# The second table of a graph network made within the first convolution's loop

## The chip, the cores and the metric

The kernel runs on one core of a Trainium2 chip. The metric is device time of one launch in microseconds (us). Five engines work side by side, each on its own queue in order: PE (TensorE) multiplies matrices, DVE (VectorE) and ACT (ScalarE) work element by element, POOL (GpSimd) issues the gathers and some element work, SP (SyncE) issues most DMAs. Some DMAs stand in ACT's queue.[...]

## The reference, cut to what matters

There are 6250 nodes of 128 features and 100000 edges sorted by their end `dst`. A layer of two graph convolutions is followed by an attention layer over the same edges.

```python
def gcn_conv(x, src, dst, ew, W, b):
    n = x.shape[0]
    deg = jax.ops.segment_sum(ew, dst, num_segments=n)
    dinv = jnp.where(deg > 0, jax.lax.rsqrt(deg), 0.0)
    norm = dinv[src] * ew * dinv[dst]
    h = x @ W
    msg = h[src] * norm[:, None]
    out = jax.ops.segment_sum(msg, dst, num_segments=n)
    return out + b
...
h = gcn_conv(x, src, dst, ew, W1, b1)      # with a loop of weight 1 at each node
h = jax.nn.relu(h)
h = gcn_conv(h, src, dst, ew, W2, b2)
x = _layernorm(x + jax.nn.sigmoid(h))
...                                        # attention over the edges, then
x = _layernorm(x + attention)
```

## The kernel before, in words

Nodes stand in 49 blocks of 128 (the last has 106). Edges stand in 49 chunks of 2048. For each convolution there is a *table* h with one row per node, scaled by the node's `dinv`. It is made by `table_of` (L323) and kept three times: as float32 rows in DRAM (`g1`, `g2`), which POOL gathers from; on chip as `hot`, the first 48 blocks split into three bfloat16 parts whose sum is the float32 value, which PE gathers from by multiplying with 0/1 masks; and transposed as the start value of the sums `acc` (the node's loop to itself), features on partitions and nodes in columns.

The chunks go through a loop. `pick` (L466) gathers a chunk's source rows: 144 mask matmuls (L475) into three PSUM tiles, which ACT scales by the edge weights into `got` (L480), and five indirect DMAs `far` on POOL for edges that found no place. It also makes the 0/1 matrices `wm` on DVE (L490, L497), of which ACT scales the far part (L514). `scatter` (L516) multiplies rows and `wm` into the PSUM tile `win` of 144 nodes, and `add_in` (L524) adds `win` to `acc` on DVE. The scatter runs one chunk behind the pick.

Beside the first convolution's loop (L846) runs `sort` (L679), which works out each edge's place, mostly on DVE and PE; its steps are dealt over the chunks. A chunk's places come back from DRAM as a row spread over the partitions (`mask<-srd`, L833), are compared on DVE (L837), and the mask is stored for the later loops (L838). In this loop `acc` is `acc1`, `win` has two buffers and `got` six.

Then comes a stage of its own. `scaled` (L309) multiplies `acc1` by `dinv`, thirteen groups of four blocks (a DMA for the row `dr`, L305, and a multiply on DVE, L307). ACT adds the bias and takes the larger of 0 and the value (L869). `table_of` then makes the second table: for each block a matmul with `w2` (L332) and a scaling copy on ACT (L333); for each group a store to `g2` (L228), the split into `hot` (ACT L318, DVE L319 and L320, POOL L321), four transposes (L339) and a copy into a second tile `acc2` (L341). Where data allow it, the scheduler sets the first of these instructions among the loop's last ones.

The second convolution's loop (L983) has an order written out by hand. It does the same gather and scatter with `g2` and `acc2`, multiplies each edge's own row on DVE (L964, L965), and carries finished nodes on to the attention's table in steps: a `Pieces` object (L444) holds one generator per group, `x1_of`, and runs a group only when the group's last node lies below `lows`, the smallest node that later chunks can touch. That generator stores its split parts to `hz` in DRAM (L425), and `hot` is loaded from `hz` in four DMAs on ACT's queue (L1174) before the third loop, the attention. The third loop has its own masks, scores and sums, and ends with the output rows.

Of the kernel before, what the change touches and what calls it, by code (L numbers as in the profile page):

```python
# [9 lines left out]
F32 = mybir.dt.float32  # L10
BF16 = mybir.dt.bfloat16
I32 = mybir.dt.int32
AF = mybir.ActivationFunctionType
# [3 lines left out]
PSUM = bass.MemoryType.PSUM  # L17
DRAM = bass.MemoryType.DRAM

P = 128  # L20
# [18 lines left out]
def gnn_kernel(ctx, tc, x, src, dst, ea, ew, W1, b1, W2, b2, fcw, fcrw, attn, loopw, out):  # L39
# [11 lines left out]
    nc = tc.nc  # L51
    N, D = x.shape
# [3 lines left out]
    NP = max(N + WC, NB * P)  # L56
    tail = N - (NB - 1) * P
    blocks = [(b, P if b < NB - 1 else tail) for b in range(NB)]
# [16 lines left out]
    GP = N // P // 4  # L75
# [31 lines left out]
    adgd = dram.tile([(NC * NL + 2) * P], F32, name="adgd")  # L107
    shd = dram.tile([NC * CC], F32, name="shd")
    hz = dram.tile([P, BP, 3, D], BF16, name="hz")
    dinvd = dram.tile([NB, P], F32, name="dinvd")  # L110
    srow = dram.tile([NC, CC], BF16, name="srow")
    srd = dram.tile([NC, GP * P], BF16, name="srd")
# [111 lines left out]
    def store_blocks(eng, table, of, b0, n):  # L224
        b1_ = min(b0 + n, NB)
        full = min(b1_, NB - 1)
        if full > b0:
            eng.dma_start(table[b0 * P : full * P, :].rearrange("(b p) f -> p b f", p=P), of[:, : full - b0, :])  # L228
        if b1_ == NB:
            eng.dma_start(table[(NB - 1) * P : N, :], of[:tail, NB - 1 - b0, :])  # L230
# [69 lines left out]
    def by_dinv(acc, b0, n, pool):  # L300

        w = min(n * P, N - b0 * P)
        row = pool.tile([P, 512], F32, name="dr")
        flat = dinvd.rearrange("b p -> (b p)")
        nc.sync.dma_start(row[:, :w], flat[None, b0 * P : b0 * P + w].to_broadcast([P, w]))  # L305
        yield
        nc.vector.tensor_mul(acc[:, b0 * P : b0 * P + w], acc[:, b0 * P : b0 * P + w], row[:, :w])  # L307

    def scaled(acc, pool):  # L309
        rows = [by_dinv(acc, b0, 4, pool) for b0 in range(0, NB, 4)]  # L310
        for r in rows:
            next(r)
            next(r, None)
# [9 lines left out]
    def table_of(inT, w, table, hot, acc, pool, wp, beside=None):  # L323


        nc.vector.memset(acc[:, N:], 0.0)
        for b0 in range(0, NB, 4):
            some = blocks[b0 : b0 + 4]
            ps = pool.tile([P, 4, D], F32, name="mm")
            st = wp.tile([P, 4, D], F32, name="rows", bufs=2)  # L330
            for b, nb in some:
                nc.tensor.matmul(ps[:nb, b - b0, :], inT[:, b * P : b * P + nb], w, start=True, stop=True)  # L332
                nc.scalar.activation(st[:nb, b - b0, :], ps[:nb, b - b0, :], AF.Copy, scale=dinv[:nb, b : b + 1])  # L333
            store_blocks(nc.sync, table, st, b0, 4)
            if hot is not None and b0 < BP:
                split_parts(hot[:, b0 : b0 + 4], st, wp)
            ps = pool.tile([P, 512], F32, name="mm")
            for b, nb in some:
                nc.tensor.transpose(ps[:, (b - b0) * P : (b - b0) * P + nb], st[:nb, b - b0, :], ident[:nb, :nb])  # L339
            n = sum(nb for _, nb in some)  # L340
            nc.scalar.copy(acc[:, b0 * P : b0 * P + n], ps[:, :n])  # L341
            if beside:
                beside()

    def normed(t, some, b0, pool):

# [169 lines left out]
    def scatter(held, ps_w):  # L516
        c, rows, wm = held
        ps = ps_w.tile([P, WC], F32, name="win")
        for g in range(G):
            n0, m = wm[g]  # L520
            nc.tensor.matmul(ps[:, n0 : n0 + m.shape[-1]], rows[g], m, start=g == 0, stop=g == G - 1)  # L521
        return ps

    def add_in(acc, c, ps):  # L524
        at = cbase_of(c)
        nc.vector.tensor_add(acc[:, ds(at, WC)], acc[:, ds(at, WC)], ps)  # L526
# [257 lines left out]
    def sort_to(steps):  # L784
        while done[0] < steps:
            done[0] += 1
            next(work)

    def steps_to(c):

        b = c // BATCH + 1
        return 2 * min(b * BATCH, NC) + b
# [28 lines left out]
        table_of(xT, w1, g1, hot, acc1, ps_mm, xp, lambda: sort_to(min(done[0] + 1, steps_to(NC - 1))))  # L821


    with tc.tile_pool(name="conv", bufs=2) as wp, tc.tile_pool(name="ps_g", bufs=3, space=PSUM) as ps_g, \
            tc.tile_pool(name="ps_w", bufs=2, space=PSUM) as ps_w:

        rows_in = {}

        def slot_rows(c):

            if c < NC:
                rows_in[c] = wp.tile([P, GP * P], BF16, name="mask", bufs=4)
                nc.sync.dma_start(rows_in[c], srd[c : c + 1, :].to_broadcast([P, GP * P]))  # L833

        def slot_masks(c):
            mask = rows_in.pop(c)
            nc.vector.tensor_scalar(mask, mask, iotap, None, op0=OP.is_equal)  # L837
            nc.sync.dma_start(masks[c], mask)  # L838
            return mask

        start, total = done[0], steps_to(NC - 1)
        sort_to(steps_to(1))
        slot_rows(0)
        slot_rows(1)
        mask, held, win = slot_masks(0), None, None
        for c in range(NC):  # L846
            to = min(total, start + -(-(total - start) * (c + 1) // max(NC - BATCH, 1)))
            to = max(to, steps_to(min(c + 2, NC - 1)))
            sort_to((done[0] + to + 1) // 2)
            if win is not None:  # L850
                add_in(acc1, c - 2, win)
            new = pick(c, mask, hot, g1, ps_g, wp, 6, 12)
            sort_to(to)
            slot_rows(c + 2)
            if c + 1 < NC:
                mask = slot_masks(c + 1)
            if held is not None:
                weigh(held)
                win = scatter(held, ps_w)
            held = new  # L860
        add_in(acc1, NC - 2, win)
        weigh(held)
        add_in(acc1, NC - 1, scatter(held, ps_w))
    sorting.close()
    edges.close()
    with tc.tile_pool(name="rows1", bufs=4) as xp:
        scaled(acc1, xp)
    for c, n in chunks512:
        nc.scalar.activation(acc1[:, c : c + n], acc1[:, c : c + n], AF.Relu, bias=cols[:, 0:1])  # L869


    leftB = ctx.enter_context(ExitStack())
    acc2 = leftB.enter_context(tc.tile_pool(name="accp2", bufs=1)).tile([P, NP], F32, name="acc2")
    with tc.tile_pool(name="tab2", bufs=2) as wp, tc.tile_pool(name="ps_t", bufs=3, space=PSUM) as ps_mm:
        table_of(acc1, w2, g2, hot, acc2, ps_mm, wp)
    rightA.close()

    with tc.tile_pool(name="conv2", bufs=2) as wp, tc.tile_pool(name="arp", bufs=2) as ap_, \
            tc.tile_pool(name="rows2", bufs=1) as rp, tc.tile_pool(name="x1p", bufs=2) as xp, \
            tc.tile_pool(name="ps_g2", bufs=4, space=PSUM) as ps_g, \  # L880
# [132 lines left out]
    with tc.tile_pool(name="look", bufs=2) as lp, tc.tile_pool(name="conv3", bufs=2) as wp, \  # L1013
# [224 lines left out]
        for b, (c0, n) in enumerate(batches):  # L1238
# [6 lines left out]
            for c in range(c0, c0 + n):  # L1245
                def beside():
                    nonlocal done, points
                    points += 1
                    to = min(more, -(-more * points // (4 * max(n - 1, 1))))
                    deal(to - done)  # L1250
                    done = to
# [19 lines left out]
        add_in(acc2, NC - 1, scatter(held, ps_w))  # L1271
        pieces.go(N, 999)
    right_r.close()
    leftB.close()
    hotp.close()


# [174 lines left out]
```

## Time and profile before

| | us |
|---|---|
| median of three runs (2057.7 to 2063.59) | 2058.34 |
| the profiled execution's own time | 2054.54 |
| its span, first to last instruction | 2052.7 |
| last sum of the first convolution added at | 736.28 |
| first sum of the second convolution added at | 810.42 |

The loop of the first convolution covers about 240 to 736 us, the second about 790 to 1290, the attention the rest. The profile's page gives busy time of each engine, a chain of waits followed back from the last instruction, and groups of instructions by source line with the tile written and the tiles read (`win<-wm,got`), the count, the mean time and the idle time before them with what ended it. "PEld" is the loading of weights, "SPq" and "ACTq" are DMAs being issued. Times in the windows are from the start of the span.

### The profile page before, as it was taken

What the parts mean: (1) busy time and instruction counts of PE and PEld (TensorE: products, weight loads), DVE (VectorE), ACT (ScalarE), POOL (GpSimd) and SP (SyncE); (2) the same over time, 40 slices, a digit from 0 to 9 for tenths busy, and PEclk for the clock granted to TensorE, in tenths of its full rate; (3) what the DMA queues carried; (4) which work ended last, traced back from release to release, by engine and by line L of the source; (5) the groups of instructions that cost most, each with busy time, mean ns of one, the idle gap of its engine ahead of it and who ended that gap; (6) DMA issues with size and microseconds to landing.
All of it is one profiled execution on the core that took longest, in us unless ns stands there. A gap on an engine that the chain in (4) does not pass through costs nothing.

```text
span 2052.7 us, 78879 instructions
## 1 busy us (share of the span) xinstructions
PE 1612.4 (79%) x33861; PEld 1460.6 (71%) x33861; DVE 1641.2 (80%) x3271; ACT 940.8 (46%) x3096; POOL 1097.1 (53%) x954
## 2 busy tenths in 40 slices
PE   2668689889798886788898885367888888989985
PEld 2456478778788765687787874257777777888885
DVE  8665988779788535899899894589989998998673
ACT  1104355454454655466676773113343434445543
POOL 5001666676675635888788881312434343535662
PEclk9767699899899977899999996568999999999998
DMA  3001343343442625687777775945656666665662
GB/s 70 24 1 37 94 127 112 101 129 95 117 115 70 209 56 193 177 246 222 239 243 244 246 235 156 134 128 139 185 163 192 171 198 171 177 178 158 182 178 67
DMA packets 260707, 306.80 MB, mean 149 GB/s; under 512 B 44121, under 2 KB 199372, under 8 KB 253299
## 3 DMA queue, kind: packets, MB, share of 16 engines
q1 hardware_dynamic: 228741, 244.80, 38.8%
q0 software_dynamic: 23520, 48.22, 11.4%
q10 hardware_dynamic: 8088, 8.65, 1.4%
q8 instruction: 268, 4.39, 0.9%
q14 instruction: 90, 0.74, 0.1%
HBM read 260.35 MB, written 41.23 MB: 147 GB/s over the span
## 4 chain that ended last, share of the span: by engine, by line
DVE 37%; PE 36%; DMA 12%; issue 8%; ACT 5%; POOL 2%; SPq 1%; DVEq 1%; POOLq 0%; ACTq 0%
PE win L521 15%; DVE wm L490 6%; PE g L475 6%; DVE sel L1081 3%; DVE put L756 2%; DMA et<-in_edge_attr_dram 2%; DMA rk<-srow 2%; DMA far<-g,sidx 2%; DMA mask<-srd 2%; DVE et L964 2%; PE rec L1192 2%; ACT got L480 2%; PE mm L332 2%; DVE ohm L751 1%; PE r L706 1%
## 5 line engine op out<-in xcount | busy, mean ns | idle before, releaser
L484 POOL DMA_INDIRECT far<-g,sidx x490 | 707.1, 1443 | 238.6 <-PE win L521 112.0
L480 ACT ACTIVATE got<-g,swt 128x128 f32<-128x128 f32 x1764 | 487.4, 380 | 350.6 <-PE g L475 152.4
L484 POOL DMA_INDIRECT far<-zd,sidx x245 | 311.4, 1271 | 449.9 <-PE win L521 329.1
L521 PE MATMUL win<-wm,got 128*128 128x144 f32 x3528 | 522.0, 306 | 12.4 <-issue 12.2
L521 PEld LDWEIGHTS win<-wm,got 128*128 128x128 f32 x3528 | 485.6, 204 | 30.6 <-issue 21.0
L475 PE MATMUL g<-hot,mask 128*32 128x128 bf16 x21168 | 384.2, 226 | 90.8 <-issue 68.4
L475 PEld LDWEIGHTS <-mask 128*32 128x32 bf16 x21168 | 327.1, 100 | 124.5 <-issue 99.9
L490 DVE TENSOR_TENSOR wm<-iota,sdst 128x1728 f32<-128x1728 f32 x147 | 286.7, 1950 | 4.4 <-DMA g<-rows 4.4
L514 ACT ACTIVATE wm<-wm,swt 128x64 f32<-128x64 f32 (+1 forms) x735 | 203.1, 357 | 99.6 <-DVE wm L497 63.4
L521 PE MATMUL win<-wm,far 128*128 128x64 f32 (+1 forms) x1470 | 186.9, 273 | 11.6 <-DMA far<-g,sidx 11.2
L521 PEld LDWEIGHTS win<-wm,far 128*128 128x128 f32 x1470 | 182.4, 195 | 12.7 <-issue 12.7
L321 POOL TENSOR_TENSOR hot<-low,hot 128x512 bf16<-128x512 f32 x24 | 42.2, 1759 | 199.7 <-DVE own L714 130.4
L1078 PE MATMUL k<-adp,rk 128*128 128x49 bf16 x2352 | 91.4, 194 | 66.3 <-DVE sel L1081 52.0
L1078 PEld LDWEIGHTS <-rk 128*128 128x128 bf16 x2352 | 83.7, 103 | 77.9 <-DVE rk L1071 42.6
L964 DVE TENSOR_TENSOR et<-et,ar_row 128x2048 f32<-128x2048 f32 (+1 forms) x49 | 111.6, 2278 | 23.7 <-DMA et<-in_edge_attr_dram 23.7
L526 DVE TENSOR_TENSOR acc<-acc,win 128x144 f32 x147 | 44.4, 302 | 96.8 <-PE win L521 85.7
L965 DVE TENSOR_REDUCE dots<-et 128x16 f32<-128x2048 f32 (+1 forms) x49 | 112.0, 2286 | 1.7
L763 PE MATMUL rec<-put,ohm 128*128 128x90 bf16 x784 | 62.0, 254 | 34.5 <-DVE put L759 33.6
L763 PEld LDWEIGHTS <-ohm 128*128 128x128 bf16 x784 | 56.9, 165 | 41.4 <-DVE put L759 33.7
L1081 DVE TENSOR_TENSOR sel<-k,ohb 128x392 f32<-128x392 f32 x98 | 83.6, 853 | 2.5 <-PE k L1078 2.1
L756 DVE TENSOR_TENSOR put<-ohg,rec 128x1360 bf16<-128x1360 bf16 x49 | 76.8, 1567 | 0.0
L709 ACT CAST own<-r 128x768 bf16<-128x768 f32 x49 | 39.7, 810 | 75.0 <-PE r L706 49.3
(390 smaller groups left out, 2375.7 us busy)
## 6 DMA issues: line engine op xcount, KB each, us to landing
et<-in_edge_attr_dram SPq DMA_DIRECT2D x97, 512.0 KB
et<-in_edge_attr_dram SPq DMA_DIRECT2D x48, 1024.0 KB
mask<-masks SPq DMA_DIRECT2D x98, 384.0 KB
rk<-srow SPq DMA_DIRECT2D x98, 256.0 KB
mask<-srd SPq DMA_DIRECT2D x49, 384.0 KB
masks<-mask SPq DMA_DIRECT2D x49, 384.0 KB
far<-g,sidx POOLq DMA_INDIRECT x490
g<-rows SPq DMA_DIRECT2D x24, 256.0 KB
```

The costliest lines, as they stand in the source:

```text
L475: nc.tensor.matmul(ps[32 * q : 32 * q + 32, g, :], mask[:, (g0 + g) * P + 32 * q : (g0 + g) * P + 32 * q + 32], hot[:, 4 * (g0 + g) + q, k ...
L480: nc.scalar.activation(got[:, g, :], ps[:, g, :], AF.Copy, scale=swt[:, c, g0 + g : g0 + g + 1])
L484: nc.gpsimd.indirect_dma_start(out=got, out_offset=None, in_=table[:, :], in_offset=bass.IndirectOffsetOnAxis(ap=sidx[:, c, g : g + 1], ax ...
L490: nc.vector.tensor_tensor(wm[:, : GP * WC].rearrange("p (g w) -> p g w", w=WC), iota[:, None, 1 : WC + 1].to_broadcast([P, GP, WC]), sdst[ ...
L514: nc.scalar.activation(m, m, AF.Copy, scale=swt[:, c, g : g + 1])
L521: nc.tensor.matmul(ps[:, n0 : n0 + m.shape[-1]], rows[g], m, start=g == 0, stop=g == G - 1)
L756: nc.vector.tensor_tensor(put[:, :, : G * F].rearrange("p t (g f) -> p t g f", f=F), ohg[:, :, :, None].to_broadcast([P, TC, G, F]), rec[: ...
L763: nc.tensor.matmul(ps, ohm[:, :, t], put[:, t, :], start=t == 0, stop=t == TC - 1)
L964: nc.vector.tensor_mul(et[:n], et[:n], ar_row[:n, None, :].to_broadcast([n, TC, D]))
L965: nc.vector.tensor_reduce(dots[:n, c, :], et[:n], AX.X, OP.add)
L1078: nc.tensor.matmul(ps[:, s, :], mk[:, s * P : (s + 1) * P], adp[:, 0, k, :NB], start=k == 0, stop=k == 2)
L1081: nc.vector.tensor_mul(sel, ps, ohb.rearrange("p b s -> p s b"))
```

## The change

A new generator `h_of` takes one group of blocks from the sums to the second table: multiply by `dinv`, bias and relu, the matmul with `w2` and the scaling copies, the store to `g2`, the transposes, and the copy back over the same columns of `acc1`. The split into three parts is on ACT and DVE, in place in the tile `hrows`, and the parts go to a new DRAM tile `hh`. A `Pieces` object in the first loop runs one step of it before `pick` and one after the loop's sort steps, when the nodes lie below the chunk's limit; what is left runs after the last sum. Then four DMAs on ACT's queue load `hot` from `hh`. The stage between the two loops is gone. `acc2` is now another name for `acc1`, which stays until the end of the attention. `win` has one PSUM buffer in place of two, and the freed bank is the pieces' own pool `ps_m`; `hrows` and `hpart` have one buffer each. The order of the second loop isn't touched.

```diff
+    hh = dram.tile([P, BP, 3, D], BF16, name="hh")
...
+    def h_of(acc, b0, n, xp, pool):
+        some = blocks[b0 : b0 + n]
+        w = sum(nb for _, nb in some)
+        at = slice(b0 * P, b0 * P + w)
+        scale = by_dinv(acc, b0, n, xp)
+        next(scale)
+        yield
+        next(scale, None)
+        yield
+        nc.scalar.activation(acc[:, at], acc[:, at], AF.Relu, bias=cols[:, 0:1])
+        yield
+        st = xp.tile([P, 4, D], F32, name="hrows", bufs=1)
+        ps = pool.tile([P, 4, D], F32, name="mm")
+        for b, nb in some:
+            nc.tensor.matmul(ps[:nb, b - b0, :], acc[:, b * P : b * P + nb], w2, start=True, stop=True)
+            nc.scalar.activation(st[:nb, b - b0, :], ps[:nb, b - b0, :], AF.Copy, scale=dinv[:nb, b : b + 1])
+        store_blocks(nc.sync, g2, st, b0, n)
+        yield
+        ps = pool.tile([P, 512], F32, name="mm")
+        for b, nb in some:
+            nc.tensor.transpose(ps[:, (b - b0) * P : (b - b0) * P + nb], st[:nb, b - b0, :], ident[:nb, :nb])
+        nc.scalar.copy(acc[:, at], ps[:, :w])
+        if b0 < BP:
+            m = min(n, BP - b0)
+            part = xp.tile([P, 4, 3, D], BF16, name="hpart", bufs=1)
+            nc.scalar.copy(part[:, :m, 0, :], st[:, :m])
+            yield
+            left = st[:, :m]
+            nc.vector.tensor_sub(left, left, part[:, :m, 0, :])
+            nc.vector.tensor_copy(part[:, :m, 1, :], left)
+            nc.vector.tensor_sub(part[:, :m, 2, :], left, part[:, :m, 1, :])
+            nc.sync.dma_start(hh[:, b0 : b0 + m], part[:, :m])
...
-    with tc.tile_pool(name="conv", bufs=2) as wp, tc.tile_pool(name="ps_g", bufs=3, space=PSUM) as ps_g, \
-            tc.tile_pool(name="ps_w", bufs=2, space=PSUM) as ps_w:
+    with tc.tile_pool(name="conv", bufs=2) as wp, tc.tile_pool(name="hp", bufs=2) as hp, \
+            tc.tile_pool(name="ps_g", bufs=3, space=PSUM) as ps_g, \
+            tc.tile_pool(name="ps_w", bufs=1, space=PSUM) as ps_w, tc.tile_pool(name="ps_m", bufs=1, space=PSUM) as ps_m:
...
+        pieces = Pieces(lambda b0, n: h_of(acc1, b0, n, hp, ps_m))
         start, total = done[0], steps_to(NC - 1)
...
             if win is not None:
                 add_in(acc1, c - 2, win)
+            pieces.go(lows[max(c - 1, 0)], 1)
             new = pick(c, mask, hot, g1, ps_g, wp, 6, 12)
             sort_to(to)
+            pieces.go(lows[max(c - 1, 0)], 1)
             slot_rows(c + 2)
...
         add_in(acc1, NC - 1, scatter(held, ps_w))
+        pieces.go(N, 999)
+        for b0 in range(0, BP, GP):
+            nc.scalar.dma_start(hot[:, b0 : b0 + GP], hh[:, b0 : b0 + GP])
     sorting.close()
     edges.close()
-    with tc.tile_pool(name="rows1", bufs=4) as xp:
-        scaled(acc1, xp)
-    for c, n in chunks512:
-        nc.scalar.activation(acc1[:, c : c + n], acc1[:, c : c + n], AF.Relu, bias=cols[:, 0:1])
-    leftB = ctx.enter_context(ExitStack())
-    acc2 = leftB.enter_context(tc.tile_pool(name="accp2", bufs=1)).tile([P, NP], F32, name="acc2")
-    with tc.tile_pool(name="tab2", bufs=2) as wp, tc.tile_pool(name="ps_t", bufs=3, space=PSUM) as ps_mm:
-        table_of(acc1, w2, g2, hot, acc2, ps_mm, wp)
-    rightA.close()
+    acc2 = acc1
...
     right_r.close()
-    leftB.close()
+    rightA.close()
     hotp.close()
```

## The prediction

> **What bounds the kernel now.** I read the page first (span, busy time, chain of waits), then the busy time by stage, then the chain inside the first convolution's loop and at its end, and last the instructions in order of time around 736 us, where the changed stage begins.
>
> ```profile
> span 2052.7 us, 78879 instructions
> PE 1612.4 (79%) x33861; PEld 1460.6 (71%) x33861; DVE 1641.2 (80%) x3271; ACT 940.8 (46%) x3096; POOL 1097.1 (53%) x954
> DVE 37%; PE 36%; DMA 12%; issue 8%; ACT 5%; POOL 2%; SPq 1%; DVEq 1%; POOLq 0%; ACTq 0%
> ```
>
> No engine is full; the chain changes between DVE and PE. The stages differ, though (columns: stretch, its length, busy time and instructions of each engine, PE clock, DMA share, GB/s):
>
> ```profile
> 261.00:661.00 400.00, 347.83 (x7795) 320.73 (x7794) 331.27 (x703) 206.69 (x722) 269.59 (x194) 0.93 0.37 107
> 661.00:737.00 76.00, 65.55 (x1509) 62.62 (x1509) 37.48 (x59) 45.53 (x158) 50.33 (x40) 0.93 0.55 158
> 737.00:791.00 54.00, 39.08 (x145) 27.31 (x145) 14.46 (x28) 29.45 (x75) 13.84 (x12) 0.60 0.23 70
> 791.00:811.00 20.00, 12.19 (x446) 11.50 (x446) 15.80 (x12) 9.72 (x38) 16.82 (x12) 0.81 0.75 266
> ```
>
> Row 1 is the first convolution's loop with the sort beside it: PE 87%, DVE 83%, ACT 52% busy. Row 3 is the second table, 54 us in which DVE does 14 us and PE runs at 0.60 of its clock. Row 4 is the start of the second convolution.
>
> ```profile
> 736.28 0.30 DVE L526 TENSOR_TENSOR acc<-acc,win 128x144 f32 x1 [4.05 <-PE win L521]
> 739.10 0.49 PE L332 MATMUL mm<-w,acc 128*128 128x128 f32 x2 [0.54 <-ACT rows L333]
> 790.38 0.34 SPq L975 DMA_DIRECT2D mask<-masks  x1
> 790.67 1.96 DVE L490 TENSOR_TENSOR wm<-iota,sdst 128x1728 f32<-128x1728 f32 x1 [4.44 <-DMA g<-rows]
> 810.42 0.30 DVE L526 TENSOR_TENSOR acc<-acc,win 128x144 f32 x1
> ```
>
> The last sum of the first convolution is added at 736.3, the first one of the second at 810.4: 74.1 us with no sum added. The 739.10 line shows why the table is slow: each block's matmul waits for ScalarE to have emptied the block before. The 790 lines show that gathers, masks and edge rows start only when the last table rows have landed. In the loop before it, the chain of waits (230 to 676 us, then pieces of the later windows) reads:
>
> ```profile
> by line: PE win L521 22.0%; DVE wm L490 12.5%; DVE put L756 9.8%; DMA mask<-srd 6.8%; PE g L475 6.5%; DVE ohm L751 5.5%; issue 5.2%; PE rec L763 3.0%; PE r L706 2.9%; DVE wm L497 2.4%; DVE ohg L753 2.3%; POOL hot L321 1.8%; DVE own L714 1.7
> ...
> 677.23 7.78 DMA dr<-dinvd
> 693.68 6.04 DMA mask<-srd
> 785.77 4.29 DMA g<-rows
> ```
>
> Summing that chain's pieces from 236 to 676 us gives DVE 47%, PE 38%, mask loads 7%. The two loads at 677 and 693 are stalls at the loop's end: the thirteen dr loads of L305 stand in SP's queue among the mask loads.
>
> [...] That is the wait at 739.10, and it stays in the changed kernel: its order of instructions has each block's matmul (new L362) waiting for the ScalarE copy (L363) of the block before. [...]0.60 in row 3, 0.93 in row 1; table matmuls moved into the loop are cheaper. [...] The trace has no such load alone; its small store at 785.77 took 4.29 us[...], and I use that for stores at this place.
>
> **The change, part by part.** Times are against the profiled execution, 2054.5 us (span 2052.7 and 1.8 around it); the median of the runs is 2058.3, 3.8 more.
>
> 1. *The stage between the convolutions goes, and a tail takes its place.* Call the end of the loop T0. Of thirteen groups eleven can run in the loop (a group goes on when its nodes lie below the chunk's lowest); the last two, of three and two blocks, come after it. By the order of the built program and its waits: at T0 SP issues mask, edge rows, mask, edge rows (2.8 MB) and only behind them the rows of the first left group. Three quarters of the table (3.5 MB) are already on the way on ACT's queue. 6.3 MB at 357 GB/s, which the table's reload at the second convolution's end reached between 1239 and 1244 us, are 17 us, begun about 6 us before T0. ACT stands at `got` of the new loop's first chunk in the midst of the left group, so that waits for mask and table too: about T0+8. Its rows land at T0+13. hrows and hpart have one buffer: DVE's L376 writes over hrows, waits for that store, and has the edge products (2.29+2.29 us each chunk) and a wm (1.95) around it: done at T0+19. Then group two: scale, store and landing (4), split (1), store of the parts (3): T0+27. The last quarter is issued there[...]. Then pick of chunks 0 and 1 (2.2 each) and scatter 0 (4.4): first sum at about T0+40. The table's gathers need the last rows (T0+23) and five descriptors of about 1.3 us: ready by T0+32, hidden. So 74 becomes 40: minus 34. Bounds: 30 if the stores aren't held by the edge rows (minus 44), 60 as in rival D (minus 14). The waiting h_i loads share a semaphore with the last quarter and come after it; DVE's copy of them stands ahead of the first sum: 4 us more at most.
>
> 2. *The dr stalls go.* Scatters started at 668.1, 675.0, 685.1, 695.9 and 707.6, then every 6.33 us. Four steps took 39.5 instead of 25.3: 14 us, of which some is the last masks' own round trip. Minus 12 (8 to 14). In the changed order the dr loads stand one to a group.
>
> 3. *The loop takes the work.* Per group DVE gets a multiply (L307 0.69), two subtractions (0.68, 0.69 as L422, L424) and a cast (0.43): 2.49, times 11 is 27 us. PE gets per block 0.47 for the matmul's two passes and 0.27 for the transpose, times 44 is 33 us. ACT gets 0.75 + 4 x 0.37 + 0.59 + 0.72 = 3.5, times 11 is 39 us, beside an ACT half idle, so as work hidden; as a hand-over it isn't (rival C). At the chain's shares the loop grows by 27 x 0.47 + 33 x 0.38 = 25 us; at the engines' busy shares by 27 x 0.83 + 33 x 0.87 = 51. I take 34, nearer the lower end, since PE's and DVE's additions of one group can lie beside each other. Below 8 it can't well be: PE would have to be over 92% busy; above 65, see C. SP gets three more DMAs per group, two of them waiting for ACT or DVE with mask loads behind them; four mask buffers hide that, and 30 us of mask waits are there already. DVE's L376 waits for a store (4.3 us); in the changed order it stands about a chunk behind the matmul (10 us), hidden; uncovered it would be up to 4 a group.
>
> 4. *One buffer for win instead of two.* A scatter now waits for the sum before it. In the trace a scatter started ahead of that sum in eight of 48 chunks, by 0.2 to 4.8 us, 21 us in all; 10 of it are the chunks of the dr stalls. 0 to 11 us; I take 3, since the gathers of the next chunk are put in between.
>
> 5. *One tile for both sums, no memset, POOL's 12 splits (1.15 us) gone:* nothing; POOL waited there. The second and third convolution keep their order and waits.
>
> Sum: -34 - 12 + 34 + 3 = -9. 2054.5 - 9 = 2045.5; with 3.8 for the median 2049.
>
> **The rivals.** *A, this sum:* 2049, own range 2034 to 2064. *B, the work falls into waits:* PE has 52 us and DVE 69 us idle in row 1; if most of the groups fall there the loop grows by 10 and the end is 2025. For it: the order was made around those waits. Against: both idle times are each other's waits, not free ones. *C, slower: the hand-over between PE and ACT inside a group.* Four matmuls each wait for ACT's copy of the last one, ACT's queue has `got` and slot copies ahead of it, and PE's gathers stand behind. In row 3 a block took 0.92 us (45 us for 49); in the loop PE may lose about that beyond its work, in all 6 us a group: 66 in place of 34, so +23: 2081. It decides from a loop longer by 46 us, 4.2 us a group. For it: PE is 87% busy already. Against: the order puts 11 to 16 gather matmuls between the four. *D, the reload takes the gain:* the same pattern stands at the end of the second convolution:
>
> ```profile
> 1291.91 11.71 SPq L425 DMA_DIRECT2D hz<-part  x1
> ...
>   ACT L1132: 19.9, 1
> ```
>
> There the last parts' store was held on SP for 11.7 us and ACT waited 19.9 us for it before the last quarter of the table could be loaded. If that comes here, 74 becomes 60 and the sum is +11: 2069. Against: there rows with narrow broadcasts fill the queue, here only the edge rows.
>
> **How the numbers follow.** A 0.45, B 0.17, C 0.24, D 0.14. No change means within 0.3%, 6 us, which is what a measurement of this kernel can tell. A gives 0.28 faster, 0.11 same, 0.06 slower; B 0.17 faster; C 0.02 same, 0.22 slower; D 0.01 faster, 0.03 same, 0.10 slower. Sum: faster 0.46, same 0.16, slower 0.38. The range 2018 to 2082 leaves about 0.2 outside.
>
> **What would show it.** Right: no stretch without DVE work over some 10 us between the convolutions; first sum of the second convolution about 40 us after the last of the first; the loop's scatters some 0.8 us further apart; no dr stall at its end. Wrong: PE idle before new L362 or L368 for ACT (C), ACT waiting over 10 us for the last parts' store (D), or DVE waiting at L376 for the g2 store.

## The result, and the profile after

The changed kernel takes 2042.14 us (median of four runs, 2035.73 to 2045.0) beside 2060.97 for the kernel before in the same set: a ratio of 0.9911, 95% interval 0.9883 to 0.9939. The profiled execution took 2041.63 us, its span is 2039.7; that of the kernel before was 2054.54 and 2052.7. So the span lost 13.0 us. The two medians of the set lie 18.8 us apart, and the interval puts the change between 12.6 and 24.1 us.

Where it went is read off the sums, which both kernels add chunk by chunk (line numbers ahead of the new generator are one higher in the new file, those behind it 35 to 40 higher: L526 is now L562):

| stretch | before | after | difference |
|---|---|---|---|
| start to the sum of chunk 0 | 261.3 | 259.5 | -1.8 |
| chunk 0 to chunk 39 | 404.8 | 417.0 | +12.2 |
| chunk 39 to chunk 47 | 65.8 | 60.5 | -5.3 |
| chunk 47 to chunk 48, the loop's last | 4.4 | 9.4 | +5.0 |
| to the first sum of the second convolution | 74.1 | 40.7 | -33.4 |
| to the last sum of all | 1222.7 | 1221.6 | -1.1 |
| to the end of the span | 19.6 | 31.0 | +11.4 |

The head of the page, then the windows of the same stages as before (length, busy us of PE, PEld, DVE, ACT, POOL, PE clock, DMA share, GB/s):

```profile
span 2039.7 us, 78861 instructions
PE 1592.0 (78%) x33861; PEld 1440.6 (71%) x33861; DVE 1647.7 (81%) x3285; ACT 940.1 (46%) x3097; POOL 1088.1 (53%) x942
```

```profile
261.00:661.00 400.00, 350.73 (x7586) 318.96 (x7577) 338.00 (x720) 227.53 (x767) 263.16 (x188) 0.96 0.43 126
661.00:747.00 86.00, 75.11 (x1737) 70.00 (x1736) 46.44 (x72) 48.91 (x177) 59.96 (x43) 0.98 0.57 164
747.00:788.00 41.00, 18.81 (x481) 16.21 (x482) 18.83 (x19) 13.94 (x50) 14.28 (x14) 0.63 0.61 193
```

The page's totals hardly differ; the stages do. The stage of 54 us with little work has shrunk to row 3. In the loop ScalarE does 21 us more in 400, and the TensorE clock is 0.96 in place of 0.93.

The boundary, in order of time from the trace of the changed kernel (start, duration, engine, instruction, and in brackets the idle time before it with what ended it):

```profile
746.34 0.30 DVE L562 TENSOR_TENSOR acc<-acc,win 128x144 f32 x1 [8.45 <-PE win L557]
...
754.38 0.37 SPq L229 DMA_DIRECT2D g<-hrows  x1
...
760.64 0.55 DVE L376 TENSOR_TENSOR hrows<-hrows,hpart 128x384 f32<-128x384 f32 x1
...
764.82 0.37 ACT L363 ACTIVATE hrows<-mm,dinv 128x128 f32<-128x128 f32 x1 [8.30 <-DVE hpart L378]
...
768.66 0.32 SPq L379 DMA_DIRECT2D hh<-hpart  x1
...
770.30 0.33 ACTq L907 DMA_DIRECT2D hot<-hh  x1
...
775.80 4.99 PE L511 MATMUL g<-hot,mask 128*32 128x128 bf16 x180 [8.70 <-DMA hot<-hh]
...
785.19 0.70 DVE L936 CAST h_f<-h_i 128x1040 f32<-128x1040 int32 x1 [16.59 <-DMA h_i<-in_dst_dram]
...
787.08 0.30 DVE L562 TENSOR_TENSOR acc<-acc,win 128x144 f32 x1
```

Read from top to bottom it is the predicted chain: the first left group's rows are stored, VectorE's edge products delay L376, the second group waits for L378 (8.30 us), the last quarter of the table is loaded when its parts have landed, and TensorE goes on with it 5.5 us after the issue. VectorE stands still for 16.6 us of this, until the loads of `h_i` have landed; its two operations on them stand ahead of the first sum, which so comes 1.9 us after the scatter's last matmul has ended.

The end of the two kernels, VectorE and SyncE, first before, then after:

```profile
2033.10 0.30 DVE L526 TENSOR_TENSOR acc<-acc,win 128x144 f32 x1 [0.98 <-PE win L521]
2034.42 0.48 DVE L1286 TENSOR_TENSOR off<-sdst,fpart 128x240 f32<-128x240 bf16 x2 [1.02 <-PE agg L437]
```

```profile
2008.69 0.30 DVE L562 TENSOR_TENSOR acc<-acc,win 128x144 f32 x1 [0.97 <-PE win L557]
...
2017.45 0.26 SPq L231 DMA_DIRECT2D out_dram<-fin  x1
2020.19 0.48 DVE L1321 TENSOR_TENSOR off<-sdst,fpart 128x240 f32<-128x240 bf16 x2 [3.80 <-DMA out_dram<-fin]
```

`off` is the first step of the final check, which tests whether the planned places held for all edges and whose result a branch reads as the last thing of the program. Before, it ran right behind the last sum, in the wait for the last output group's rows. Now it waits until the last output rows have landed, and the branch behind it comes later. The diff doesn't touch these lines. What has moved is memory: `acc2` lay below the tiles of the third loop on one side of memory, and without it they lie 25.6 KB lower. By the built program's addresses the pool of the check and of the rare path behind it spans 56832 to 185024 in both kernels, with `off` at its start; `fin`, the tile of the output rows, lies at 198560 before and at 172960 after. So the check's pool now lies over `fin`, though `off` itself doesn't, and the pool's first instruction waits for fin's stores.

### The profile page after: what moved, and what is told of

It reads as the page before. It is cut to its first block, busy times and chain, and to the rows that moved or that the text cites. A ratio compares the mean times of both kernels' runs of the same rounds, so it can differ in the third digit from the quotient of the medians.

```text
span 2039.7 us, 78861 instructions
## 1 busy us (share of the span) xinstructions
PE 1592.0 (78%) x33861; PEld 1440.6 (71%) x33861; DVE 1647.7 (81%) x3285; ACT 940.1 (46%) x3097; POOL 1088.1 (53%) x942
## 3 DMA queue, kind: packets, MB, share of 16 engines
q0 software_dynamic: 23520, 48.22, 11.4%
## 4 chain that ended last, share of the span: by engine, by line
DVE 25%; PE 22%; DMA 10%; issue 6%; ACT 3%; SPq 1%; POOL 1%; DVEq 0%; ACTq 0%; POOLq 0%
PE win L557 11%; PE g L511 4%; DVE wm L526 4%; DVE sel L1116 3%; DMA et<-in_edge_attr_dram 3%; DMA far<-g,sidx 2%; DVE et L999 2%; DMA rk<-srow 2%; PE rec L1227 2%; ACT got L516 1%; DVE asr L1117 1%; PE r L1257 1%; DVE put L1223 1%; PE k L1113 1%; DMA mask<-masks 1%
## 5 line engine op out<-in xcount | busy, mean ns | idle before, releaser
L557 PE MATMUL win<-wm,got 128*128 128x144 f32 x3528 | 512.2, 302 | 7.8 <-issue 7.2
L557 PEld LDWEIGHTS win<-wm,got 128*128 128x128 f32 x3528 | 477.3, 201 | 22.5 <-issue 13.2
L526 DVE TENSOR_TENSOR wm<-iota,sdst 128x1728 f32<-128x1728 f32 x147 | 286.9, 1951 | 0.4 <-issue 0.3
L557 PEld LDWEIGHTS win<-wm,far 128*128 128x128 f32 x1470 | 181.4, 194 | 21.1 <-issue 18.5
L1113 PEld LDWEIGHTS <-rk 128*128 128x128 bf16 x2352 | 82.8, 102 | 78.9 <-DVE rk L1106 42.9
L562 DVE TENSOR_TENSOR acc<-acc,win 128x144 f32 x147 | 44.3, 302 | 92.6 <-PE win L557 78.6
L322 POOL TENSOR_TENSOR hot<-low,hot 128x512 bf16<-128x512 f32 x12 | 28.5, 2376 | 155.0 <-DVE own L750 130.4
L745 ACT CAST own<-r 128x768 bf16<-128x768 f32 x49 | 39.8, 811 | 73.0 <-PE r L742 55.2
```

The costliest lines, as they stand in the source:

```text
L526: nc.vector.tensor_tensor(wm[:, : GP * WC].rearrange("p (g w) -> p g w", w=WC), iota[:, None, 1 : WC + 1].to_broadcast([P, GP, WC]), sdst[ ...
L1113: nc.tensor.matmul(ps[:, s, :], mk[:, s * P : (s + 1) * P], adp[:, 0, k, :NB], start=k == 0, stop=k == 2)
```

## The experiments

Chips differ here (the kernel before took 2056.06 us on one and 2434.66 on another), so runs that are compared by time are compared as ratios to the kernel before on the same chip; distances inside a trace are set beside those of the table.

### 1. The final check in a pool of its own

```diff
-    with tc.tile_pool(name="slow", bufs=1) as sl, ...
+    with tc.tile_pool(name="last", bufs=1) as la, tc.tile_pool(name="slow", bufs=1) as sl, ...
-        off = sl.tile(...); wide_ = sl.tile(...); any_ = sl.tile(...)
+        off = la.tile(...); wide_ = la.tile(...); any_ = la.tile(...)
```

> The changed kernel with the final check's three small tiles in a pool of their own, so that they no longer lie in the region of the large pool for the rare path, which since the change reaches over the output tile fin. Theory (the end lost about 11 us because the check's first subtraction waits for the last output store): the check runs before the last output group, the time from the last sum to the end falls from 31.0 us to 19 to 21 us, and the run is 9 to 12 us faster than the changed kernel, about 2031 us. Rival (the end is set by the load of the check's value and the branch, whatever precedes them): the end stays within 3 us of 31.0. Everything before the last sum stays within 2 us of the changed kernel under both.

2026.72 us, ratio 0.9825 (0.9763 to 0.9886). From the last sum to the end 15.8 us in place of 31.0, better than the 19.6 of the kernel before. The loop (chunk 0 to 39 416.9) and the boundary (41.1) stay within 2 us of the changed kernel; the way from there to the last sum is 4.3 us shorter, more than expected, and not explained. In order of time, VectorE at the end of this kernel:

```profile
1992.40 0.49 DVE L1321 TENSOR_TENSOR off<-sdst,fpart 128x240 f32<-128x240 bf16 x2
...
2003.67 0.31 DVE L562 TENSOR_TENSOR acc<-acc,win 128x144 f32 x1 [0.98 <-PE win L557]
2004.09 0.28 DVE L1332 TENSOR_REDUCE any__43587<-mm 1x1 f32<-1x128 f32 x1
```

The same instruction now runs without a wait, 11 us ahead of the last sum. `off` still lies at 56832; only the pool that it belongs to is another, and that pool no longer reaches over `fin`. The end was lost to the shared memory, and the rival, an end that is fixed by load and branch, falls. The run gains more than 12 us because the check also moved ahead, which only its own pool allowed, and by the 4.3 us.

### 2. The reload held back

ScalarE writes one value of each quarter of `hot` from the last `win` first, so the reload can't start before the last scatter's end.

```diff
+        win = scatter(held, ps_w)
+        nc.scalar.copy(hot[0:1, 0:BP:GP, 0, 0], win[0:1, 0:4])
+        add_in(acc1, NC - 1, win)
-        add_in(acc1, NC - 1, scatter(held, ps_w))
```

> The changed kernel with the four reloads of hot held back until the last scatter has written win (ScalarE writes one element of each quarter of hot from win first). Theory (the 3.5 MB of the reload collide with the last chunk's far gathers): the sum of chunk 48 comes about 5 us after that of chunk 47 instead of 9.4, the gathers of the last chunk land in under 4 us instead of 10, and the last sum comes 5 to 9 us earlier; of this at least half is kept at the first sum of the second convolution. Rival (the last chunk's scatter is late because of the edge rows, the masks or the pieces, not the reload): the last sum moves by less than 2 us. Second rival: the gain is there at the last sum but is lost whole at the first sum of the second convolution, since the reload now ends later.

2052.41 us, one run, with the kernel before at 2067.13 on that chip. The last step is 8.9 us (9.4 in the changed kernel), and the boundary is 45.5 in place of 40.7. TensorE at the last scatter, first in the changed kernel, then here:

```profile
743.08 0.37 PE L557 MATMUL win<-wm,far 128*128 128x16 f32 x2 [1.82 <-DMA far<-g,sidx]
745.72 0.58 PE L557 MATMUL win<-wm,far 128*128 128x16 f32 x2 [2.27 <-DMA far<-g,sidx]
```

```profile
742.40 0.40 PE L557 MATMUL win<-wm,far 128*128 128x16 f32 x2 [0.45 <-DMA far<-g,sidx]
744.27 0.36 PE L557 MATMUL win<-wm,far 128*128 128x16 f32 x2 [1.48 <-DMA far<-g,sidx]
```

Both wait for the last gathers. GpSimd issued the last one at 735.20 in the changed kernel, and TensorE had it 10.5 us later; here it was issued at 739.70, and TensorE had it 4.6 us later. The same distance is 10.4 us in experiment 1, 9.0 in experiment 3 and 9.2 in experiment 10, where the reload is in flight, and 4.2 in experiment 4, where it comes later. So the gathers beside the reload take longer, but here GpSimd was later itself, and nothing was won at the last sum. Why it was later, with the same order of instructions on it, isn't known. The reload then came late for the new loop: TensorE waited 5.5 and 4.2 us for `hot`. Holding back is a loss.

### 3. A tile of its own for the rest of the split

```diff
-            tc.tile_pool(name="hp", bufs=2) as hp
+            tc.tile_pool(name="hp", bufs=1) as hp
-            left = st[:, :m]
-            nc.vector.tensor_sub(left, left, part[:, :m, 0, :])
+            left = xp.tile([P, 4, D], F32, name="hleft")[:, :m]
+            nc.vector.tensor_sub(left, st[:, :m], part[:, :m, 0, :])
```

> The changed kernel with a tile of its own for the rest of the split in place of the subtraction in place in hrows, dr with one buffer to make room. Theory of the prediction (the subtraction waits for the store of the rows, and the second left group waits for both): the subtraction of the first left group runs within 3 us of its rows' scaling instead of 6, and the first sum of the second convolution comes 3 to 6 us earlier against the last sum of the first. Rival (VectorE's edge products and masks hold it, not the store): less than 1.5 us.

2048.91 us, one run. At the boundary the expectation was wrong: L376 does run early (745.54, 0.7 us after the rows' store is issued), but the boundary is 47.4 us in place of 40.7. The last store of parts stands behind new neighbours on SyncE: it was ready at 756.8, was issued at 761.68 behind three loads of `h_i`, the first of which was issued only at 760.58, when GpSimd's memset of `h_i` (759.57) was done, which stands behind five gathers; and the last quarter of the table followed at 765.09. What nobody had expected is in the loop: chunk 0 to chunk 39 takes 407.5 us in place of 417.0. VectorE's waits from chunk 0 to 39 in the changed kernel (instruction, what it waited for: us in all, times, longest):

```profile
DVE own L746 <- ACT own L745: 19.8, 14, 2.3
DVE acc L562 <- PE win L557: 10.1, 9, 3.7
DVE mask L874 <- DMA mask<-srd: 9.1, 6, 2.5
DVE hrows L376 <- DMA g<-hrows: 6.5, 2, 4.0
```

The last line is the in-place subtraction that waits for the store of the rows it writes over. In this experiment's trace the line is gone; the subtraction waits 0.9 us for ScalarE. In the trace of experiment 1, whose loop is that of the changed kernel and as long (416.9 us), the waits at L376 have other names:

```profile
DVE hrows L376 <- ACT own L745: 4.4, 1, 4.4
DVE hrows L376 <- DMA g<-hrows: 2.8, 2, 2.3
DVE hrows L376 <- PE mm L368: 1.7, 1, 1.7
```

The subtraction reads ScalarE's cast (L373) and writes over rows that the store and the transposes (L368) still read, and the profile names what came last. So the store alone isn't shown to be what it costs. All waits at L376 up to chunk 39 make 8.2 us in the changed kernel, 8.9 in experiment 1 and 10.2 in experiment 2, which have the same loop, against 0.9 here.

### 4. All pieces after the loop

```diff
-            pieces.go(lows[max(c - 1, 0)], 1)     # both calls in the loop
```

> The changed kernel with no piece run inside the first convolution's loop; all thirteen groups run after the last sum. The distance between the sums of chunk 0 and chunk 39, 417.0 us in the changed kernel and 404.8 in the kernel before, gives what the pieces cost in the loop. Theory (about three quarters of the added work falls into waits and a quicker TensorE clock; one buffer for win costs 0 to 5): 403 to 409 us. Rival, the prediction's (the loop grew by 34, and something else in the change made it 25 shorter): about 380 us. The stretch from the last sum to the first sum of the second convolution should grow from 40.7 us to 90 or more.

2132.61 us, one run; boundary 129.3. Chunk 0 to 39 takes 415.4, above the expected band. The steps show where: chunk 38 takes 21.4 us and 13.5 in the other kernels' traces of this pace. There TensorE stood 7.80 us before a scatter's last matmuls, waiting for a gather, and on GpSimd two gathers took over 10 us to issue:

```profile
641.11 10.77 POOL L520 DMA_INDIRECT far<-g,sidx  x1 [0.30 <-PE g L511]
652.18 10.41 POOL L520 DMA_INDIRECT far<-g,sidx  x1 [0.30 <-PE rec L799]
```

Apart from these 7.9 us the stretch is 407.4, 2.6 more than in the kernel before. So the run speaks against a loop that had become 25 us shorter by itself, but its own stall keeps it from being a clean base; the last experiment gives a better one.

### 5 to 9. Two chips on which the kernel takes 2430 us

These ran on two other chips, on which the kernel before took 2434.66 and 2432.43 us in place of 2060; distances can't be set beside the first traces there.

> The kernel before with one PSUM buffer for win in the first convolution in place of two, nothing else. Prediction's term: plus 3 us, between 0 and 11. From the trace of the kernel before, scatters that started ahead of the previous sum overlapped it by 21 us in eight chunks; if that overlap is needed, the distance from the first sum to the last (475.0 us) grows by about 10; if the gathers put in between fill it, by 0 to 3. Expected: 0 to 3 up to chunk 39 (404.8 us in the kernel before).

```diff
-            tc.tile_pool(name="ps_w", bufs=2, space=PSUM) as ps_w:
+            tc.tile_pool(name="ps_w", bufs=1, space=PSUM) as ps_w:
```

2414.24 us, one run. No trace of the unchanged kernel from that chip stands beside it, but the next run's kernel has two buffers and differs from the unchanged one only in loads that are issued from chunk 39 on. It takes 504.6 us from chunk 0 to 39, and this one 499.7: one buffer costs nothing at this pace (one run each; the last experiment repeats it).

> The kernel before with the thirteen loads of dr for the second table on ScalarE's queue in place of SyncE's, so that no mask load stands behind them. Theory of the prediction: the stalls at chunks 41 and 42 (14.1 and 11.1 us in place of 6.3 to 8) go, and the distance from the sum of chunk 39 to that of chunk 48 falls from 70.2 us by 8 to 12. Second theory (GpSimd issues five gathers a chunk, about 7.6 us at its back-to-back pace, against 6.3 us of a chunk at the loop's end; without the stalls it becomes late): the last chunk's step grows from 4.35 us to over 6, and the fall is only 4 to 8. No reload of the table runs in this kernel, so a long last step here can't come from it.

```diff
-        rows = [by_dinv(acc, b0, 4, pool) for b0 in range(0, NB, 4)]
+        rows = [by_dinv(acc, b0, 4, pool, nc.scalar) for b0 in range(0, NB, 4)]   # queue of the DMA
```

2438.69 us, one run. Chunk 39 to 48 took 87.3 us here and 82.8 in the one before it, whose loads are still on SyncE: at this slower pace moving them won nothing, and the question isn't decided.

> The changed kernel with two edits: the final check's tiles in a pool of their own (as in the first experiment), and the rest of the split computed into the group's own dr tile, which has been used up by then, in place of hrows. The order of TensorE, ScalarE and GpSimd is that of the changed kernel. Theory (in the loop the first subtraction waits for the store of the rows to g2, because it writes over what is being stored): the first sum to that of chunk 39 falls from 417.0 to 407 to 410 us, near the 407.5 of the run with a tile of its own; the stretch between the convolutions stays at 38 to 43; the run is 7 to 12 us faster than the run with the check alone: 2015 to 2020 us. Rival (that run's shorter loop came from its other order or from its single dr buffer): over 414 us at chunk 39.

```diff
-            left = st[:, :m]
-            nc.vector.tensor_sub(left, left, part[:, :m, 0, :])
+            left = row.rearrange("p (b d) -> p b d", d=D)[:, :m]      # row: the group's dr tile
+            nc.vector.tensor_sub(left, st[:, :m], part[:, :m, 0, :])
```

2415.22 us, ratio 0.9911 (0.9876 to 0.9945), and in a second set on the other chip:

> The kernel with the two edits again (the final check's tiles in a pool of their own, the rest of the split in the used-up dr tile), since in the last set the kernel before itself took 2435 us instead of 2060, so that no distance could be set beside the first two traces. If the kernel before takes about 2060 us here: first sum to that of chunk 39 407 to 410 us in place of 417.0 (theory: the subtraction no longer waits for the store), against over 414 (rival); the stretch between the convolutions 38 to 43; the last sum to the end 15 to 17; the run 2013 to 2022 us, a ratio of 0.977 to 0.982 to the kernel before.

2418.35 us, ratio 0.9929 (0.9900 to 0.9957). Both times faster than the kernel before. The interval of experiment 10, the same kernel on a quicker chip, covers both. The boundary took 50.6 us in the first of these traces, not the 38 to 43 that were expected.

> The changed kernel without the four loads of hot from hh: the second convolution then gathers from the first one's table, so that its values are others while the work stays the same. Theory one (the reload's 3.5 MB delay the last chunk's gathers): the last gather lands within 5 us instead of 10.4, and the step of chunk 48 falls from 9.4 to 4 to 6 us. Theory two (GpSimd itself is late): the step stays at 8 or more. The stretch to the first sum of the second convolution loses the wait for the last quarter: it falls from 40.7 to 30 to 36 us, if the gathers of the table's rows are not late themselves.

```diff
-        for b0 in range(0, BP, GP):
-            nc.scalar.dma_start(hot[:, b0 : b0 + GP], hh[:, b0 : b0 + GP])
```

2428.51 us, one run. The last step is 4.69 us, and with the reload in experiment 7 on the same chip also 4.69: where the loop's end runs at 8 us a chunk, GpSimd's gathers are in time and the reload costs the last chunk nothing. The boundary is 38.6 us against 50.6 with the reload; but the two kernels differ in the split as well, so not all of the 12 us is the reload's.

### 10. The two edits beside each other

> The kernel with the two edits once more, on whatever chip this set gets, to stand beside the next run on the same chip. If the kernel before takes about 2060 us here: first sum to that of chunk 39 407 to 410 us in place of 417.0 (theory: the subtraction no longer waits for the store), against over 414 (rival); the run 2013 to 2022 us.

2025.86 us, ratio 0.9889 (0.9811 to 0.9968), the kernel before at 2056.06. Chunk 0 to 39 takes 410.9 us, just outside the expected band and below the rival's 414, and 6.1 less than the changed kernel and than experiment 1. VectorE no longer waits for a store at L376; all its waits there make 0.8 us. The boundary is 48.4 us, as in experiment 3 and for the same reason, so what the loop gained is given back at its end, and the run misses the 2013 to 2022 us. Experiment 1's kernel, with one edit, is faster than the kernel before by a ratio of 0.9825; the intervals of the two overlap, so a gain by the second edit isn't shown, and one edit is simpler.

### 11. The pieces' work doubled

```diff
+            nc.tensor.matmul(...)        # each once more
+            nc.tensor.transpose(...)     # each once more
+            nc.vector.tensor_copy(part[:, :m, 1, :], left)      # six times more
+            nc.scalar.copy(part[:, :m, 0, :], st[:, :m])        # five times more
```

> The last kernel with the pieces' work doubled on three engines, with nothing new computed: each matmul with w2 and each transpose twice on TensorE, six more casts of hpart on VectorE, five more on ScalarE, in each group. Up to chunk 39 nine groups run, so TensorE gets some 23 us more, VectorE 23, ScalarE 28. The prediction's price of such work (the chain's shares 0.47 and 0.38, or the busy shares 0.83 and 0.87): the distance from the first sum to that of chunk 39 grows by 19 to 40 us over the run with the two edits. Rival (the work falls into waits that are there anyway, as the first comparison suggests): by less than 10 us.

2067.24 us, one run on the chip of experiment 10. Windows from chunk 0 to chunk 39, each from its own trace: the kernel before, the kernel with the two edits, this one:

```profile
261.29:666.12 404.83, 352.66 (x7849) 325.55 (x7850) 335.39 (x711) 209.17 (x731) 272.68 (x196) 0.93 0.37 106
```

```profile
257.27:668.14 410.87, 371.10 (x8041) 338.70 (x8041) 355.07 (x747) 236.57 (x798) 269.94 (x196) 0.95 0.43 125
```

```profile
258.38:693.78 435.40, 382.16 (x8202) 348.30 (x8199) 370.26 (x798) 259.85 (x847) 285.19 (x195) 0.95 0.40 117
```

The first dose of work put 19.7 us on VectorE, 18.4 on TensorE and 27.4 on ScalarE, and the stretch grew by 6.0. The second put 15.2, 11.1 and 23.3 on them, and it grew by 24.5. By the prediction's two prices the first should have cost 16 (chain's shares) to 32 (busy shares), the second 11 to 22. So the price isn't a constant, and neither dose cost what the two prices say. With the first dose VectorE's idle time went from 69.4 to 55.8 us and TensorE's from 52.2 to 39.8: the work fell into waits. With the second they rose again, to 65.1 and 53.2. Idle time was left, and yet the work didn't fall into it. New waits stand in the list (VectorE's mask compare behind TensorE's win, 12.8 us in two places). This run lengthens the hand-overs inside a group as well as the work, so the 24.5 isn't the price of busy time alone; which of the two made it isn't shown.

### 12. The kernel before with one win buffer and the dr loads on ScalarE's queue

The edits are those of experiments 5 and 6 together.

> The kernel before with one buffer for win and the dr loads on ScalarE's queue. The two edits act at different places: to chunk 39 only the buffer, from chunk 39 on also the loads. If the kernel before takes about 2060 us here: first sum to that of chunk 39 404.8 to 408 us if the single buffer costs 0 to 3 as the prediction took it, up to 415 if the overlap of 21 us is needed; from chunk 39 to 48 58 to 62 us in place of 70.2 if the dr stalls go and nothing takes their place, 62 to 66 if GpSimd's gathers are late next, with a last step over 6 us in place of 4.35.

2054.41 us, one run, with the kernel before at 2056.06. Chunk 0 to 39 takes 403.7 us (404.8 with two buffers): the single buffer costs nothing there. Chunk 39 to 48 takes 65.9 in place of 70.2: with the loads gone from SyncE 4.3 us are won, not 8 to 12, for chunk 41 still takes 12.6. The last step is 4.7, so GpSimd isn't late in this kernel, and the second theory is not borne out here. Experiment 4 bears on it too. It issues none of these loads before the loop's end, neither on SyncE nor on ScalarE, and runs no piece there: chunk 39 to 48 takes 63.7 us, and the last step is 6.7, of which TensorE waits 1.3 for the last gather. That is what the second theory expected. But it is one run, behind a stall of its own.

## Why the prediction was right, and where its steps were not

The predicted total, 9 us less, stands against 12.9 measured on the profiled executions (2049 against 2042 in the median; the interval of the change, 12.6 to 24.1 us, lies above 9). It is right in sign and near in size, but only the boundary among its large terms is shown to have been right; the loop was far off, the dr stalls are open, and one term was missing.

- *The boundary (minus 34).* Measured minus 33.4, 40.7 us against "about T0+40", and the chain link by link: T0+8 for the first rows' store (measured 8.0), second group from T0+19 (18.5), last quarter issued at T0+27 (24.0). TensorE went on with it at T0+29.5. The links came up to 3 us early, and the way from there to the first sum took 11.3 us, where the prediction's two picks and scatter make 8.8. The load of the last quarter took 5.5 us from its issue until TensorE went on with it, with other loads in flight; what T0+40 holds for it was the author's estimate, shown by no trace beforehand. Experiment 1 repeats the boundary with 41.1. Of the signs named ahead one didn't come: VectorE has a stretch of 16.6 us without work. Rival D's held-up reload didn't come in the changed kernel. Two kernels that only moved the split show how near it was: 47.4 and 48.4, by a store behind other loads on SyncE.
- *The loop (plus 34).* This term is the failed one. To chunk 39, where nine of the eleven groups run, the loop grew by 12.2 where 28 were due (34 x 9/11); 6 to 9.5 of that is the split done in place (experiments 10 and 3), and the pieces' work with all its other hand-overs cost some 6 (experiment 10 against the kernel before; 7.2 against experiment 12). Three traces of one and the same loop differ by 2 us here. The step that failed is "I take 34, nearer the lower end ... Below 8 it can't well be: PE would have to be over 92% busy". It priced the work by the share each engine has in the chain or in the time, as if waits were a fixed part, and it put nothing for a change of the loop's other work. Rival B had the mechanism of the waits.

  The clock came beside it. TensorE's busy time was to grow by 27 us (33 x 9/11) and grew by 13.9 in the changed kernel and 18.4 in experiment 10, at a granted clock of 0.96 and 0.95 in place of 0.93, and it was 90.3% busy in experiment 10. A matmul with `w2` took 275 ns in the median in the changed kernel's loop (L362, 88 of them), and 421 in the stage of the kernel before (L332, 98). On one chip this stretch ran at 0.92 without pieces (experiment 4) and at 0.94 to 0.97 with them (1 to 3), on another at 0.94 without (12) and 0.95 with them (10).

  Rival C's sign came too, but small: up to chunk 39 TensorE waited for ScalarE's copies ahead of L362 in six places, 5.0 us in all. For more work of the same kind experiment 11 shows a higher cost, but not its price.
- *The store behind L376.* "It stands about a chunk behind the matmul (10 us), hidden" was wrong in four groups of the eleven: the changed kernel's trace has 13.2 us of waits for that store at L376, 6.5 of them up to chunk 39. The fallback of "up to 4 a group" was the right size (4.0 the longest), for four groups rather than eleven. The other readers of the rows, which it also waits for, are not in the prediction.
- *The dr stalls (minus 12).* Chunk 39 to 47 lost 5.3, with the work of two groups in it. Experiment 12 gives 4.3 up to chunk 48 for loads that are moved to another queue, and chunk 41's step stays long with them. Experiment 4, which has neither these loads nor pieces there, takes 57.1 us up to chunk 47, 8.8 less than the kernel before. So the size of this term stays open between the two.
- *The last chunk (not in the sum).* Its step grew by 5.0 us. It waits for the last gathers. Two causes are seen, gathers that take 9.0 to 10.5 us beside the reload in place of 4.2 to 4.6, and gathers issued late; experiment 2 took the first away and met the second. How the 5 us divide stays open. In experiment 10, with the reload in flight, the step was 6.6.
- *One buffer for win (plus 3).* Nothing, by experiments 12 and 5. The overlap of 21 us was there but not needed.
- *"The second and third convolution keep their order and waits."* True of the loops (-1.1 us), false of the end: 11.4 us by memory that was shared anew, shown by experiment 1. The prediction costed "one tile for both sums" at nothing and looked only at the instructions that use the tile, not at what moves into its place.

From chunk 0 to the loop's last sum the prediction's terms make plus 25 (34 + 3 - 12); measured is plus 11.9, with the last chunk's 5.0 in it. The 13 us by which this is better and the 11.4 lost at the end nearly cancel, and so the total came out near. That is luck: the sum had neither of them.

## What to carry to other kernels

When a large tile goes, everything above it in memory moves (here by 25.6 KB): look for later first uses whose region now lies over a tile that is still being stored, above all at the end, where nothing covers a wait (here 11.4 us). Work added to a loop of two engines that wait for each other can cost far less than its busy time (6.0 us here for 19.7 on one and 18.4 on the other), and more of the same can cost more than its busy time (24.5 for 15.2 and 11.1, with longer hand-overs), so one price doesn't serve for both; one more dose, run as an experiment, tells on which side one is. And an instruction that wrote in place over a tile (L376) waited for what still read the tile, 14.9 us in the changed kernel, 13.2 of them for the DMA that stores it: compute the result into another tile, then look again at the order of the queue that the later store stands in.

## What the runs showed of the hardware

On two of the chips the kernel before took 2435 and 2432 us, 18% more than on the others. In the trace of experiment 7 from one of them, TensorE's gather matmuls show idle time before them that nothing named ended:

```profile
L511 PE MATMUL g<-hot,mask 128*32 128x128 bf16 x21168 | 570.6, 246 | 298.5 <-issue 265.6 <-DMA hot<-hh 22.0 <-DMA mask<-masks 4.3
```

In the changed kernel's trace from a quicker chip (without the two edits of experiment 7) the same group has:

```profile
L511 PE MATMUL g<-hot,mask 128*32 128x128 bf16 x21168 | 387.4, 225 | 77.1 <-issue 58.3 <-DMA hot<-hh 8.7 <-DMA mask<-masks 5.6
```

Busy and idle time of this one group are 405 us more together, against 387 us more in the span, while the mean granted clock is 0.844 against 0.893. The cause wasn't tried.

The issue of a gather on GpSimd, 1.04 us in the median of the first loop, took up to 8.05 us there in the changed kernel, 7.15 in the one before and 10.77 in experiment 4. During those 10.77 us VectorE ran additions, comparisons and products of two tensors without a pause, as it did during most of the next 10.41, up to a wait of 7.83 us.

The changed kernel's trace has 490 such gathers in its first two loops, and they can be sorted by what VectorE did in the first 0.94 us of each. Where VectorE was idle (52 gathers) the issue took 0.94 to 0.95 us. Where it ran a reduction, which reads one tensor (48), the issue took the same. Where it ran float32 operations on two tensors (169) the issue took 2.20 us in the median, and with bfloat16 operations on two tensors (65) 1.23 in the median and 8.05 at the most.

So the long issues go with operations on two tensors. That these hold the issue up is read from the traces, not shown by an edit. If it is so, VectorE work that is added to fill its waits can make gathers late, which may be why GpSimd was late in experiment 2. That was not tried.
